# The first product of each seven-product down pair goes into the third bank and is copied; the fourth pair of the last but one batch takes the seven-product form

## The chip, the cores and the metric

The kernel runs on one core of one Trainium2 chip. The metric is the device time of one execution in microseconds (us), as the median of several runs. The core has a matrix engine (PE, with its weight loads listed as PEld), a vector engine (DVE), a scalar engine (ACT), a general engine (POOL) and the DMA queues, most of which are issued from SP. Matmul results land in PSUM, which the program allots in banks of 128 partitions by 512 float32.

## The reference: a gated feed-forward layer with quantised activations and ternary down weights

Inputs are `x` (4 x 1024 x 512, float32), a condition vector per batch (4 x 128), `norm_w` (512 x 128), `up_w` (4096 x 512) and `down_w` (512 x 2048). Cut to what matters:

```python
scale = cond @ norm_w.T + 1.0
h = x * (scale[:, None, :] * rsqrt(mean(x * x) + EPS))
val, gate = split(h @ up_w.T)                 # 2 x 2048 columns
h = val * gelu(gate)
hq = round(h * 127 / max|h| per token) ...    # int8 grid per token
wq = round(down_w / mean|down_w|) in -1, 0, 1 # ternary
y = hq @ wq.T * scales + x
```

## The kernel before, in words

There are four batches of 1024 tokens. Work is written out by hand: the program order of each engine's instructions is the order in which that engine runs them, and the framework puts in the semaphores. The hidden width of 2048 is cut into NJ = 16 blocks of 128. Batch 0 takes the plain up product; batches 1, 2 and 3 take the up product in a seven-product form, one `slot` for each block, so that slots are numbered g = 16 to 63. A slot's up matmuls are 512 wide (L580).

The down product of a batch is done while a later batch is in its slots. It works on tiles of 128 tokens. A `Pair` (L812 and after) takes two tiles, one of each half h of the batch, for the same tile number a (0 to 3), and forms the 2 x 2 block product over the two halves of the 2048 hidden columns and the two halves of the 512 output columns. It takes seven products of eight matmuls each, 256 wide (L851), rather than the 32 matmuls 512 wide of the plain form `down_mm` (L800). The methods are:

- `sum1` and `sums` form four sums of the tokens' blocks on DVE (L827, L834 to L836).
- `first` runs three products: B11, T1 and B21. `third` runs T2, `fourth` runs B22 and T3, `fifth` runs T4. In what follows these are the products' names, with the pair's number a in brackets where it is needed: T1(3).
- Three PSUM banks k1, k2 and k3 are used. The first product is needed in both halves of k1. `first` puts it into the right half and ACT copies it to the left half (L859). `third` has an ACT copy from k1 to k2 (L868) and `fourth` one inside k2 (L877). `onto` (L891) is the DVE instruction that scales a bank, or half a bank, and adds it to the token's `x`.

Batches 0 and 1 are brought down as pairs in slots j = 10 to 13 (`DOWN`) of the batch that follows each, b = 1 and b = 2: eight pairs, whose `first` stands at the slot's start (`early`). Batch 2 is brought down at the very end: pairs 0, 1 and 2 in the seven-product form (`old_first`, `old_third`, `old[a].fourth()`, `old[a].fifth()`), their sums made in the slots j = 10 to 12 of the last batch, and tile number 3 in the plain form, 32 matmuls 512 wide in three pieces of 8, 16 and 8 (`down_mm(b - 1, ...)`). Between these stand the steps of the last batch's own quantisation, for the eight pieces i of 2 blocks of one half h, in the list `work`: `quant_scale` on DVE (L772), and then either a rounding on DVE (L776) or two on ACT (`quant_up` L780 and `quant_down` L784). The last batch's own down product (`po_end`, L800) needs these pieces and ends the kernel.

Of the kernel before, what the change touches and what calls it, by code (L numbers as in the profile page):

```python
# [50 lines left out]
def glu_quant_kernel(  # L51
# [68 lines left out]
    def t_view(b):  # L120
        v = R[:, b % 2].bitcast(F16)[:, : NA * C_ALL * 2 * HALF]
        return v.rearrange("p (a c l k t) -> p a c l k t", a=NA, c=C_ALL, l=2, k=2)
# [16 lines left out]
    def s_tile(g):  # L139


        if g >= NJ:
            return SXY[:, (g + 1) % 2]
        return S_more if g % 3 == 2 else SXY[:, g % 3]

    def h_slots(g, n=1):
        s = g % NSLOT
        return H[:, s : s + n]
# [7 lines left out]
    def bank(tag, bufs, shape=None, name=None):  # L156
        return psum.tile(shape or [P, TOK], F32, name=name or tag, tag=tag, bufs=bufs)
# [416 lines left out]
    def product(c, g, ps, start, stop):  # L574
        s = s_tile(g)[:, PLACE[c]]
        s = s.rearrange("p w (k f) -> p w k f", k=2)
        tv = t_view(g // NJ)
        o = ps.rearrange("p (a t) -> p a t", t=P)
        for n, (w, l, k) in enumerate(TERMS):
            PE.matmul(  # L580
                o, s[:, w, k, :], tv[:, :, c, l, k, :],
                start=start and n == 0, stop=stop and n == len(TERMS) - 1,
                skip_group_check=True,
            )
# [210 lines left out]
    def down_mm(b, h, a, po, js, y0=0, y1=2):  # L795

        q = q_view(b)
        n = NJ // 2
        for j in js:
            PE.matmul(  # L800
                po.rearrange("p (y c o) -> p y c o", c=2, o=P),
                q[:, a, h, j],
                wd8[:, :, j // n, j % n, :, y0:y1].rearrange("p c o y -> p y c o"),
                start=j == 0, stop=j == NJ - 1,
            )
# [6 lines left out]
    class Pair:  # L812
# [23 lines left out]
            DVE.tensor_tensor(self.s[4], a12, self.s[2], ALU.subtract)  # L836
            self.s[3] = a21

        def product(self, w, name, bank, half, start, stop, both=False):


            w = w.rearrange("p (j t) -> p j t", t=P)
            t = w_block(name)
            n = NJ // 2
            for j in range(n):
                m, po = t[:, :, j], bank[:, half * HALF : (half + 1) * HALF]
                po = po.rearrange("p (c o) -> p c o", c=2)
                if both and j == 0:
                    m = m.rearrange("p (y c) o -> p y c o", y=1).to_broadcast([P, 2, 2, P])
                    po = bank.rearrange("p (y c o) -> p y c o", y=2, c=2)  # L850
                PE.matmul(  # L851
                    po, w[:, j], m, start=start and j == 0, stop=stop and j == n - 1,
                    skip_group_check=True,
                )

        def first(self, banks):
            self.banks = k1, _, k3 = banks
            self.product(self.part(0, 0), "B11", k1, 1, True, True, True)
            ACT.copy(k1[:, :HALF], k1[:, HALF:])  # L859
            self.product(self.s[1], "T1", k3, 0, True, True)  # L860
            self.product(self.part(0, 1), "B21", k1, 0, False, True)

# [386 lines left out]
    def add_pieces(dve, act, b, s, pieces, at):  # L1249
        for i, h in pieces:  # L1250
# [9 lines left out]
            cost = 1.29 + (0.8 if (i, h) in BY_VECTOR else 0)  # L1260
            dve.add(at, cost, go, (slot, "z" if (i, h) in BY_VECTOR else "x"))

    def old_places(a):

        if a == 0:
            v = wpool.tile([P, 2, D], F32, name="sq_0", tag="xn", bufs=1)
            u = wpool.tile([P, 4, HALF], F32, name="sr_0", tag="xt", bufs=1)
            return v[:, 0], v[:, 1], u.rearrange("p n d -> p (n d)")[:, :D]
        if a == 1:
            v = wpool.tile([P, C_ALL, 2, HALF], F16, name="sq_1", tag="nx", bufs=1)  # L1270
            v = v.rearrange("p c l d -> p (c l d)").bitcast(F32)
            return [v[:, n * D : (n + 1) * D] for n in range(3)]
        v = h_slots(B * NJ, 2).rearrange("p s h t -> p (s h) t")
        return [v[:, n] for n in range(3)]

    state = {}
    for b in range(1, B):
# [45 lines left out]
        for j in range(NJ):  # L1323
            g = b * NJ + j
            down = b + 1 < B and j in DOWN
            if down:
                pair, a = pairs[j], DOWN[j]
                xrs = [down_load(b - 1, h, a) for h in range(2)]
            early_sums, late_sums = D_SUM_AT.get((b, j), ((), ()))
            left = SLOT_US + PAIR_US * down - OWN_US + 0.4  # L1330
            more = D_SUM_US * len(late_sums) + 0.7 * (j + 1 == min(DOWN) and b + 1 < B)
            left -= D_SUM_US * len(early_sums) + more
            mine = {p: [sum(c[e] for _, c in steps.get((j, p), ())) for e in range(2)] for p in "xyz"}
            left -= sum(mine[p][0] for p in "xyz")
            act_left = {"x": 2.7, "y": 2.2 if down else 1.1, "z": 0}

            def run(p):
                nonlocal left
                for f, _ in steps.get((j, p), ()):
                    f()  # L1340
                if p == "x":
                    cap = min(left, 3.9 - mine["x"][0] - (0 if down else mine["y"][0] + more))
                    left -= cap - dve.run((j, p), cap)
                elif p == "z":
                    left = dve.run((j, p), left)
                if p != "z":
                    act.run((j, p), act_left[p] - mine[p][1])

            def early():
                if down:  # L1350
                    pair.first([po_bank(f"po_{b}_{a}_{n}") for n in range(3)])
                    pair.sums()
                d_sums(early_sums)

            def next_pair():
                if b + 1 < B and j + 1 in DOWN:
                    pairs[j + 1] = Pair(b - 1, DOWN[j + 1])
                    pairs[j + 1].sum1(h_slots(g + 1)[:, 0, 0])

            def more_sums():  # L1360
                next_pair()
                d_sums(late_sums)

            mid = [nothing] * 3
            if j + 1 == min(DOWN):
                mid[0] = more_sums
            if down:
                mid = [lambda: (pair.third(xrs, dq), d_sums(late_sums)), lambda: (pair.fourth(), next_pair()), lambda: (loads(), pair.fifth())]

            def loads():  # L1370
                if NJ + 2 <= g + 2 < B * NJ:
                    s_load_x(g + 2)
                if NJ + 2 <= g + 1 < B * NJ:
                    s_load_y(g + 1)


            def late():
                if b == 1 and j + 1 == min(DOWN):

                    banks = [po_bank(f"po_set_{n}") for n in range(3)]  # L1380
                    PE.matmul(
                        banks[1].rearrange("p (a t) -> p a t", t=P),
                        s_tile(g + 1)[:, 0, 0, :P], t_view(b)[:, :, 0, 0, 0, :],
                        start=True, stop=True,
                    )

            if b + 1 == B and j in DOWN and DOWN[j] < 3:
                pairs[DOWN[j]] = Pair(b - 1, DOWN[j])
                places = old_places(DOWN[j])
                pairs[DOWN[j]].sum1(places[0])  # L1390
                pairs[DOWN[j]].sums(*places[1:])
            if j == 4:
                token_turn(b - 1, am)
            if j == 5:
                bring_dq = token_undo(b - 1, dq)
            if j == 6:
                bring_dq()
            if j == NJ - 1:
                get_ready()
            elif b == 1 and j == 0:  # L1400
                get_ready()
            slot(g, lambda: run("x"), lambda: run("y"), lambda: run("z"), early, mid, late)
            if not down:
                loads()
# [18 lines left out]
            xr = down_load(b - 1, h, a)  # L1423
        old_x[h, a] = xr

    old = [pairs[a] for a in range(3)]

    def old_banks(a):
        if a % 2 == 0:
# [3 lines left out]
    def old_first(a):  # L1433
        old[a].first(old_banks(a))

    def old_third(a):
        old[a].third([old_x[h, a] for h in range(2)], state[b - 1])
# [55 lines left out]
        f()  # L1493
    last_loads()

    pos = [bank("AE"[h], 2, name=f"po_{b}_3_{h}") for h in range(2)]
    down_mm(b - 1, 0, 3, pos[0], range(NJ // 2))
    old[2].fourth()
    for f in work[2:7]:
        f()  # L1500
    down_mm(b - 1, 0, 3, pos[0], range(NJ // 2, NJ))
    down_mm(b - 1, 1, 3, pos[1], range(NJ // 2))
    old[2].fifth()
    down_mm(b - 1, 1, 3, pos[1], range(NJ // 2, NJ))
    for f in work[7:11]:
        f()
    for h in range(2):
        down_end(b - 1, h, 3, pos[h], old_x[h, 3], state[b - 1])
    for f in work[11:]:
        f()  # L1510
    work = [f for _, f in token_scale(1, am)] + [lambda: token_turn(b, am, 1, 2)]
# [56 lines left out]
```

## Time and profile before

| | |
|---|---|
| median of 3 runs | 731.27 us (730.51 to 731.33) |
| profiled execution, its own time | 730.43 us |
| span of that execution, first to last instruction | 728.6 us |
| granted TensorE clock | 1.000 |
| busy: PE, DVE, ACT, POOL | 99%, 80%, 54%, 27% of the span |

The profile counts times from the span's start. A matmul's own duration in it (272 ns for 256 columns, 379 ns for 512) is longer than the distance to the next, since matmuls are pipelined; what a row of eight costs is read from the start of one group to the start of the next. In a line of the timeline stand the start in us, the length, the engine, the source line, the operation, the tile written and the tiles read, the count, and in brackets the idle time before it with what ended it.

### The profile page before, as it was taken

How to read it: one execution, taken by the hardware profiler on the slowest of the kernel's cores; microseconds unless marked ns; L12 is line 12 of the kernel's file. 1: busy time of each engine (PE TensorE's matmuls, PEld its weight loads, DVE VectorE, ACT ScalarE, POOL GpSimd, SP SyncE). 2: the span in 40 equal slices, each digit the busy share in tenths (PEclk: the TensorE clock that was granted, in tenths of full speed). 3: DMA queues.
4: the chain of work that ended last, by engine and by line, in shares of the span. 5: the costliest groups of instructions: out<-in, count | busy, mean ns of one | idle time of the engine just before them, and what ended most of it. 6: DMA issues, size and time to landing. Idle time of an engine off the chain costs nothing.

```text
span 728.6 us, 10140 instructions
## 1 busy us (share of the span) xinstructions
PE 719.9 (99%) x3661; PEld 358.8 (49%) x3661; DVE 581.2 (80%) x819; ACT 396.3 (54%) x629; POOL 196.1 (27%) x207
## 2 busy tenths in 40 slices
PE   7999999999999999999999999999999999999998
PEld 3544444444444446655444445665444444445744
DVE  7877889975698899788689897787678888755897
ACT  6868876772336674444335676543433665332274
POOL 1379887775100033440000030360020000000100
PEclk9999999999999999999999999999999999999999
DMA  6759999988444654876735646866934555452253
GB/s 236 251 172 303 291 273 249 254 199 230 117 102 102 131 155 130 180 186 159 181 101 103 131 101 174 202 144 163 230 96 102 90 114 104 101 102 89 89 188 115
DMA packets 203982, 117.30 MB, mean 161 GB/s; under 512 B 165382, under 2 KB 174487, under 8 KB 203932
## 3 DMA queue, kind: packets, MB, share of 16 engines
q1 hardware_dynamic: 203642, 116.33, 63.8%
q8 instruction: 28, 0.46, 0.2%
q10 hardware_dynamic: 290, 0.33, 0.1%
q14 instruction: 22, 0.18, 0.1%
HBM read 54.22 MB, written 23.09 MB: 106 GB/s over the span
## 4 chain that ended last, share of the span: by engine, by line
PE 96%; DVE 1%; DMA 1%; ACT 0%; issue 0%; SPq 0%; DVEq 0%
PE A L580 34%; PE E L580 17%; PE pg L595 10%; PE pv L595 10%; PE B L580 9%; PE po L851 8%; PE po_end L800 4%; PE po L800 1%; DMA H<-in_x_dram 1%; DMA SXY<-H 1%; PE po_B L851 0%; PE ptx L941 0%; PE pv L638 0%; DVE R L949 0%; PE pw L323 0%; PE pg L638 0%
## 5 line engine op out<-in xcount | busy, mean ns | idle before, releaser
L580 PEld LDWEIGHTS <-SXY 128*128 128x128 f16 x2016 | 197.2, 98 | 232.3 <-issue 0.6
L580 PE MATMUL A<-R,SXY 128*128 128x512 f16 x1152 | 266.2, 379 | 0.0
L580 PE MATMUL E<-R,SXY 128*128 128x512 f16 x576 | 140.0, 379 | 0.1
L678 DVE SCALAR_TENSOR_TENSOR H<-A,sg,t 128x512 f32<-128x512 f32 x48 | 36.0, 750 | 73.4 <-PE A L580 73.2
L730 POOL PARTITION_ALL_REDUCE am<-R x8 | 14.4, 1794 | 230.7 <-DVE R L716 230.7
L772 DVE TENSOR_TENSOR H<-H,am 128x1024 f32<-128x1024 f32 x64 | 76.2, 1216 | 0.0
L595 PEld LDWEIGHTS <-SXY 128*128 128x128 f16 x486 | 47.5, 98 | 57.4 <-DMA SXY<-H 0.8
L691 ACT ACTIVATE t<-t,sg 128x512 f32<-128x512 f32 x48 | 34.6, 721 | 70.1 <-DVE t L688 69.9
L580 PE MATMUL B<-R,SXY 128*128 128x512 f16 x288 | 70.0, 379 | 0.0
L714 DVE TENSOR_REDUCE gm<-H 128x512 f32<-128x1024 f32 x56 | 69.0, 1232 | 1.0
L595 PE MATMUL pg<-R,SXY 128*128 128x512 f16 x252 | 57.8, 379 | 0.3 <-DMA SXY<-H 0.3
L851 PE MATMUL po<-wd,R 128*128 128x256 fp8e4 (+1 forms) x448 | 56.8, 275 | 0.0
L595 PE MATMUL pv<-R,SXY 128*128 128x512 f16 x234 | 54.4, 379 | 0.0
L851 PEld LDWEIGHTS <-R 128*128 128x128 bf16 (+1 forms) x480 | 47.0, 98 | 12.8
L675 ACT ACTIVATE t<-B,sg 128x512 f32<-128x512 f32 x48 | 33.0, 688 | 36.4 <-PE B L580 36.4
L484 POOL TENSOR_SCALAR ssq<-ssq 128x2 f32<-128x2 f32 x12 | 3.6, 299 | 176.8 <-ACT xt L514 124.1
L658 ACT COPY t<-A 128x512 f32<-128x512 f32 x48 | 28.0, 583 | 39.5 <-PE A L580 39.2
L666 ACT COPY B<-A 128x512 f32<-128x512 f32 x48 | 27.4, 572 | 39.0 <-PE A L580 38.6
L780 ACT ACTIVATE H<-H 128x1024 f32<-128x1024 f32 x38 | 39.9, 1050 | 14.1 <-DVE H L772 14.1
L670 ACT COPY v<-E 128x512 f32<-128x512 f32 x48 | 28.1, 586 | 31.3 <-PE E L580 27.8
L716 DVE TENSOR_TENSOR R<-R,gm 128x512 f32<-128x512 f32 x56 | 41.9, 749 | 1.3
L697 DVE SCALAR_TENSOR_TENSOR H<-v,sg,t 128x512 f32<-128x512 f32 x48 | 36.6, 762 | 7.4 <-ACT t L691 7.4
(207 smaller groups left out, 972.5 us busy)
## 6 DMA issues: line engine op xcount, KB each, us to landing
SXY<-s_dram SPq DMA_DIRECT2D x57, 256.0 KB, 3.2
s_dram<-SXY SPq DMA_DIRECT2D x18, 384.0 KB, 3.3
H<-in_L_cond_up_w_dram SPq DMA_DIRECT2D x13, 512.0 KB, 5.6
SXY<-s_dram SPq DMA_DIRECT2D x39, 128.0 KB, 3.3
xr<-in_x_dram SPq DMA_DIRECT2D x19, 256.0 KB, 3.5
out_dram<-xr SPq DMA_DIRECT2D x19, 256.0 KB, 2.6
H<-in_x_dram SPq DMA_DIRECT2D x8, 512.0 KB, 7.9
R<-in_L_cond_down_w_dram SPq DMA_DIRECT2D x8, 512.0 KB, 7.1
```

What stands on the lines that cost most here:

```text
L580: PE.matmul(o, s[:, w, k, :], tv[:, :, c, l, k, :], start=start and n == 0, stop=stop and n == len(TERMS) - 1, skip_group_check=True,)
L595: PE.matmul(ps, a[k // 2][:, w, k % 2, :], XP[:, l, k, h * TOK : (h + 1) * TOK], start=n == 0, stop=n == len(terms) - 1,)
L675: ACT.activation(cur["t1"], pb, AF.Gelu, scale=gain(g, 1))
L678: DVE.scalar_tensor_tensor(h_half(g - 1, 0), prev["A"], gain(g - 1, 0), prev["t1"], ALU.mult, ALU.mult)
L691: ACT.activation(prev["t2"], prev["t2"], AF.Gelu, scale=gain(g - 1, 1))
L697: DVE.scalar_tensor_tensor(h_half(g - 1, 1), prev["v"], gain(g - 1, 0), prev["t2"], ALU.mult, ALU.mult)
L714: DVE.tensor_reduce(gm[0], v, AX.X, ALU.max, apply_absolute_value=True)
L716: return [largest, lambda: DVE.tensor_tensor(m, m, gm[0], ALU.max)]
L772: DVE.tensor_tensor(v, v, r.to_broadcast([P, 2, TOK]), ALU.mult)
L780: ACT.activation(v, v, AF.Copy, bias=MAGIC)
L800: PE.matmul(po.rearrange("p (y c o) -> p y c o", c=2, o=P), q[:, a, h, j], wd8[:, :, j // n, j % n, :, y0:y1].rearrange("p c o y -> p y c o"),
L851: PE.matmul(po, w[:, j], m, start=start and j == 0, stop=stop and j == n - 1, skip_group_check=True,)
```

## The change

In the eleven pairs, and in a new twelfth, the first product goes 256 wide into the right half of the third bank k3, and ACT copies it from there into both halves of k1 with one instruction 512 wide. T1 then goes into the left half of the same bank k3, as it did before. The one matmul in a pair that was 512 wide is gone. Since k1 is then never started by a matmul in a pair, one more matmul is issued, once, in the slot before the first pair.

Tile number 3 of batch 2 becomes a fourth pair. Its sums are made in slot j = 13 of the last batch, in places left over from the other pairs. Its products stand at the end of the kernel in the place of the three pieces of the plain form.

```diff
-        def product(self, w, name, bank, half, start, stop, both=False):
+        def product(self, w, name, bank, half, start, stop):
...
-                if both and j == 0:
-                    m = m.rearrange("p (y c) o -> p y c o", y=1).to_broadcast([P, 2, 2, P])
-                    po = bank.rearrange("p (y c o) -> p y c o", y=2, c=2)
...
         def first(self, banks):
             self.banks = k1, _, k3 = banks
-            self.product(self.part(0, 0), "B11", k1, 1, True, True, True)
-            ACT.copy(k1[:, :HALF], k1[:, HALF:])
+            self.product(self.part(0, 0), "B11", k3, 1, True, True)
+            m1 = k3[:, HALF:].rearrange("p (y o) -> p y o", y=1).to_broadcast([P, 2, HALF])
+            ACT.copy(k1.rearrange("p (y o) -> p y o", y=2), m1)
             self.product(self.s[1], "T1", k3, 0, True, True)
             self.product(self.part(0, 1), "B21", k1, 0, False, True)
...
-        v = h_slots(B * NJ, 2).rearrange("p s h t -> p (s h) t")
-        return [v[:, n] for n in range(3)]
+        if a == 2:
+            v = h_slots(B * NJ, 2).rearrange("p s h t -> p (s h) t")
+            spare.append(v[:, 3])
+            return [v[:, n] for n in range(3)]
+        return [wpool.tile([P, D], F32, name="sq_3", tag="sc", bufs=1), *spare]
...
                     banks = [po_bank(f"po_set_{n}") for n in range(3)]
-                    PE.matmul(
-                        banks[1].rearrange("p (a t) -> p a t", t=P),
-                        s_tile(g + 1)[:, 0, 0, :P], t_view(b)[:, :, 0, 0, 0, :],
-                        start=True, stop=True,
-                    )
+                    for bank in banks[:2]:
+                        PE.matmul(
+                            bank.rearrange("p (a t) -> p a t", t=P),
+                            s_tile(g + 1)[:, 0, 0, :P], t_view(b)[:, :, 0, 0, 0, :],
+                            start=True, stop=True,
+                        )
...
-            if b + 1 == B and j in DOWN and DOWN[j] < 3:
+            if b + 1 == B and j in DOWN:
                 pairs[DOWN[j]] = Pair(b - 1, DOWN[j])
...
     last_loads()
 
-    pos = [bank("AE"[h], 2, name=f"po_{b}_3_{h}") for h in range(2)]
-    down_mm(b - 1, 0, 3, pos[0], range(NJ // 2))
+    old_first(3)
     old[2].fourth()
     for f in work[2:7]:
         f()
-    down_mm(b - 1, 0, 3, pos[0], range(NJ // 2, NJ))
-    down_mm(b - 1, 1, 3, pos[1], range(NJ // 2))
+    old_third(3)
     old[2].fifth()
-    down_mm(b - 1, 1, 3, pos[1], range(NJ // 2, NJ))
     for f in work[7:11]:
         f()
-    for h in range(2):
-        down_end(b - 1, h, 3, pos[h], old_x[h, 3], state[b - 1])
+    old[3].fourth()
+    old[3].fifth()
     for f in work[11:]:
         f()
```

More of the change, by code (lines that the diff above doesn't have):

```diff
@@ L1261, in add_pieces @@
             dve.add(at, cost, go, (slot, "z" if (i, h) in BY_VECTOR else "x"))
+    spare = []
     def old_places(a):
@@ L1267, in old_places @@
             u = wpool.tile([P, 4, HALF], F32, name="sr_0", tag="xt", bufs=1)
-            return v[:, 0], v[:, 1], u.rearrange("p n d -> p (n d)")[:, :D]
+            u = u.rearrange("p n d -> p (n d)")
+            spare.append(u[:, D:])
+            return v[:, 0], v[:, 1], u[:, :D]
         if a == 1:
@@ L1424, in old_load @@
         old_x[h, a] = xr
-    old = [pairs[a] for a in range(3)]
+    old = [pairs[a] for a in range(NA)]
     def old_banks(a):
```

## The prediction

> **What bounds the kernel now.** I read the page's busy times and chain first, then the timeline of one pair in the middle, then the timeline of the end, then the stretches of the end.
>
> ```profile
> PE 719.9 (99%) x3661; PEld 358.8 (49%) x3661; DVE 581.2 (80%) x819; ACT 396.3 (54%) x629; POOL 196.1 (27%) x207
> ...
> PE 96%; DVE 1%; DMA 1%; ACT 0%; issue 0%; SPq 0%; DVEq 0%
> ```
>
> PE bounds nearly everything, so a matmul saved is time saved, and a time in which PE waits is time lost. First, PE at the start of a middle pair (b = 1, a = 0), and ACT in the same stretch:
>
> ```profile
> 274.07 1.14 PE L851 MATMUL po<-wd,R 128*128 128x512 fp8e4 x8
> 275.06 1.04 PE L851 MATMUL po<-wd,H 128*128 128x256 fp8e4 x8
> ```
> ```profile
> 274.62 0.72 ACT L691 ACTIVATE t<-t,sg 128x512 f32<-128x512 f32 x1 [0.71 <-DVE t L688]
> 275.26 0.36 ACT L859 COPY po<-po 128x256 f32<-128x256 f32 x1
> ```
>
> B11 takes 0.98 (274.07 to 275.06), then T1 runs on while ACT copies. The copy begins 0.20 after T1's start, takes 0.36, and is done 0.31 before B21 at 275.93. Nothing waits. Now the end, where the fourth tile's plain matmuls (L800) lie among pair 2's products; PE, ACT and DVE in turn:
>
> ```profile
> 687.92 1.89 PE L800 MATMUL po<-wd,R 128*128 128x512 fp8e4 x8
> 689.65 1.04 PE L851 MATMUL po<-wd,H 128*128 128x256 fp8e4 x8
> 690.52 1.04 PE L851 MATMUL po<-wd,R 128*128 128x256 fp8e4 x8
> 691.40 3.62 PE L800 MATMUL po<-wd,R 128*128 128x512 fp8e4 x16
> 694.85 1.04 PE L851 MATMUL po<-wd,R 128*128 128x256 fp8e4 x8
> ```
> ```profile
> 690.64 1.06 ACT L780 ACTIVATE H<-H 128x1024 f32<-128x1024 f32 x1 [2.98 <-DVE H L772]
> 691.73 1.06 ACT L784 ACTIVATE R<-H 128x1024 bf16<-128x1024 f32 x1
> 692.69 0.37 ACT L877 COPY po<-po 128x256 f32<-128x256 f32 x1
> ```
> ```profile
> 687.95 0.75 DVE L891 SCALAR_TENSOR_TENSOR SXY<-po_B,dq,SXY 128x512 f32<-128x512 f32 x1
> 688.61 0.87 DVE L891 SCALAR_TENSOR_TENSOR SXY<-po,dq,SXY 128x256 f32<-128x256 f32 x2
> 689.39 1.22 DVE L772 TENSOR_TENSOR H<-H,am 128x1024 f32<-128x1024 f32 x1
> ```
>
> The reader is to see L877. Its product T3(2) is through at 691.40, but the copy runs only at 692.69, behind the two roundings of piece 0 that stand before it in ACT's order. It costs nothing, because 16 plain matmuls (3.45) cover it until T4(2) at 694.85. DVE has no gap from 685.3 on; in the busy times by stretch it is the third engine figure:
>
> ```profile
> 700.00:710.00 10.00, 10.00 (x48) 4.54 (x47) 9.90 (x13) 6.04 (x7) 0.00 (x0) 1.00 0.32 97
> ```
>
> **Unit prices.** A product of eight 256-wide matmuls: 0.875 (685.30, 686.18, 687.05, 687.92). A 512-wide matmul: 0.216 (16 in 691.40 to 694.85). ACT's copy of 512 columns between banks:
>
> ```profile
> L666 ACT COPY B<-A x48: 570/570/579, 187.2 to 661.8; 128x512 f32<-128x512 f32 x48
> ```
>
> So 0.57. PE to ACT 0.20 as above; ACT to PE 0.05 (a cast L347 ends at 13.67, the matmul that needs it starts at 13.72).
>
> **Part 1, B11 at 256 wide.** 0.98 becomes 0.875: minus 0.105 a pair.
>
> **Part 2, the copy out of k3.** ACT now reads one half of the bank into whose other half PE wants to write T1 next. May it? No row of before has PE writing half a bank while another engine reads the other half, so both ends stay: no wait, or T1 waits for the whole copy. Nearest is a pair of readers near the start:
>
> ```profile
> 22.16 0.41 DVE L359 TENSOR_TENSOR SXY<-pw,SXY 128x256 f16<-128x256 f32 x1
> 22.61 0.59 ACT L363 COPY H<-pw 128x512 f32<-128x512 f32 x1 [0.34 <-DVE SXY L359]
> ```
>
> Both only read the bank pw and write elsewhere, and yet ACT idled 0.34 until DVE had ended. Two readers have no data to order; the program orders engines on a bank. I take the wait. Its size: 0.20 + 0.57 + 0.05 = 0.82, less 0.105, so plus 0.715 a pair.
>
> The Trainium skill, PSUM — Partial Sum Buffer, section "PSUM bank collisions raise a hardware error", speaks against this change: two engines may not touch one bank on the same partitions at once, disjoint columns included, and semaphores must guard by bank. By it T1 waits in every pair; by addresses alone it would not, and rival one's sum would hold. The L363 row agrees with the page.
>
> Seven of the eight middle pairs pay it: 5.0. ACT is free there when B11 ends (in the pair shown, the gelu ends at 275.34, and B11 is 0.22 later by the added setting matmul). The eighth (b = 1, a = 3) waits already:
>
> ```profile
> 321.66 0.50 PE L851 MATMUL po<-wd,H 128*128 128x256 fp8e4 x3 [0.59 <-DVE H L827]
> ```
>
> Its T1 starts 0.75 after B11's end because of sum1; the two waits overlap, so 0. The setting matmul adds 0.22. Middle: 5.2. Should the copy cost only the 0.36 of the narrow one, each pair is 0.21 cheaper; should a 0.72 gelu stand ahead of it each time, about 0.45 dearer.
>
> **Part 3, sums of the fourth pair.** Four DVE instructions at 0.69 = 2.75, at the start of slot 13 of the last batch. DVE is idle there for 3.76 before L678 at 647.45, so 0; without that cover up to 2.75 late on DVE. Their places are the other pairs' leftovers, and no new wait shows.
>
> **Part 4, the end, in order of time.** Bare matmul time falls: 32 x 0.216 = 6.90 becomes 7 x 0.875 = 6.12, minus 0.78. But the plain pieces were the cover.
>
> Pair 0: ACT is in a gelu from 670.11 to 670.83, so the copy runs 670.79 to 671.36 and T1(0) starts 671.41, not 670.25; shift 1.1 to 1.2. Pairs 1 and 2 add 0.715 each. B11(3) thus starts at 690.5, where 687.92 stood, and ends at 691.4.
>
> Its copy stands on ACT behind the roundings of piece 0. DVE's gapless run is moved by 1.8 with PE (its L688 waits for a slot product, 683.87 to 685.7), so L772 of piece 0 ends at 692.3, the roundings (2.2) at 694.6, the copy at 695.1. T1(3) starts 695.14: PE has waited 3.7.
>
> B21(3), then B22(2) end at 697.8. Only now can DVE do pair 2's `onto` (698.0 to 698.7), and behind it in DVE's order wait L772 for pieces 1, 2 and 3. Piece 1 ends at 699.9, its roundings at 702.2, and only then comes ACT's copy of third(3) (to 702.5). PE, through with T3(2), T2(3) and T4(2) at 700.4, waits 2.1 for B22(3).
>
> T3(3) ends at 704.3. Its copy stands behind the roundings of pieces 3 and 4; piece 4's L772 follows three `onto` on DVE and ends at 705.4, the roundings at 707.7, the copy at 708.0. T4(3), right behind T3(3) with nothing between, has waited 3.8 and ends at 708.9. That is where `po_end` starts, at 697.45 before: plus 11.4. Check: 1.1 + 2 x 0.715 + 3.7 + 2.1 + 3.8 - 0.78 = 11.4.
>
> `po_end` is gapless PE work of 27.7. It would now have its pieces with more to spare than before (half 1's first L772 at about 716 for a need at 722.7), so DVE's two more half-width `onto` (0.87 the two) and the later SP stores cost nothing. The whole 11.4 reaches the end.
>
> **Sum.** 730.43 + 5.2 + 11.4 = 747.0 for a profiled execution; the median lies 0.84 above that execution: 747.9.
>
> The Trainium skill, TensorE: Matmul & The Clock Gate, Part 1, says that PE idle for a window of about 3.4 us drops to half clock. By it, as an estimate, each of the two longest waits could cost 1.7 more, which would make 751.3. The longest PE wait of before is 1.5 and all slices have clock 1.00, so no run here shows it; the sum leaves it out.
>
> **Rivals.** *One, order by address:* T1 runs on, B21 is due 0.875 after B11 and needs 0.82, no wait. Middle: -8 x 0.105 + 0.22 = -0.6. At the end B21(3) still waits for a copy behind the roundings: 0.4 + 3.0 + 2.1 + 3.8 - 0.8 and the rest of pairs 0 to 2, about 8.8. Time 739.5. Against it: the L363 row.
>
> *Two, bank waits only:* DVE and ACT catch up during them, and the copies of the fourth pair find ACT free. 11 x 0.715 + 0.22 - 0.78 - 0.7, plus 0.20 + 0.36 + 0.05 for T4(3) behind T3(3): 738 to 739. Against it: DVE's 9.90 of 10.
>
> *Three, faster:* neither wait, because ACT takes the fourth pair's copy at once. It decides at L772 of piece 0: its roundings, 2.2, would have to be over at 689.0, when B11(3)'s copy is due, so L772 would have to end by 686.8; it ended at 690.61. Price: 12 pairs' saving is 11 x 0.105 + 0.78 - 0.22 = 1.7, of which the end lets through about 0.3, since ACT's last rounding of piece 3 of half 1 ends at 715.44 for a need at about 715.7. Between -0.9 and -1.7: 729.6 to 730.4.
>
> **How the numbers follow.** Main case 0.87; one 0.06; two 0.04; three 0.02; no change 0.01. Main alone: 12 copies at the cheap or dear end move it by -2.3 or, in the eight middle pairs, +3.6, and the end's three waits by about 2 either way, since they hang on DVE's order. Both seldom add, so 743.5 to 752.0, which leaves out the rivals and a tenth of the main case, under 2 in 10. A measurement tells 0.2% (1.5 us) from no change: faster 0.02, same 0.01, slower 0.97.
>
> **What would show it.** Right: T1's PE rows (L851) wait on ACT for about 0.6 to 0.8 in each pair; L859's successor is 0.57 long; near 691 to 708 PE stands still three times, for 3.7, 2.1 and 3.8, each until an ACT copy behind L784; `po_end` starts near 714 (708.9 + 5.2). Wrong: T1 following B11 with no gap; `po_end` starting before 706; DVE idle where I have it full.

## The result, and the profile after

The changed kernel takes 751.68 us (median of 6 runs, 749.98 to 753.74) beside 730.98 us for the kernel before (6 runs, 730.51 to 731.33). The ratio is 1.0285, with a 95% interval of 1.0269 to 1.0301: slower by 20.7 us. The profiled execution shown here has a span of 750.7 us and took 752.44 us.

The page of the kernel after, the same two parts as were shown of before, and the granted clock in 40 slices:

```profile
PE 724.5 (97%) x3686; PEld 363.2 (48%) x3686; DVE 584.9 (78%) x825; ACT 399.7 (53%) x632; POOL 195.7 (26%) x207
...
PEclk9999999999999999999999999999999999999899
...
PE 4%; ACT 0%; DVE 0%; issue 0%
```

PE's share falls from 99% to 97%, and one slice near the end shows a granted clock below 0.9. The chain that ended last now reaches back only to the end of the kernel (PE 4% in place of 96%). TensorE's own waits are therefore the view to read: PE's waits by what ended them, in total, with their number and the longest.

```profile
PE po L848 <- ACT po L857: 4.4, 6, 1.1
PE po_E L848 <- ACT po_B L857: 4.3, 2, 3.7
PE po_A L848 <- ACT po_A L875: 3.7, 1, 3.7
...
PE po L848 <- DVE H L697: 2.6, 4, 0.7
PE po_B L848 <- ACT po_A L866: 1.8, 1, 1.8
```

For the kernel before, this list has one line of a pair only, of 0.6. L857 is the copy that was L859, L866 and L875 were L868 and L877, and the products' line L851 is now L848. The four waits put down to DVE's L697 stand at T1 of other pairs and are just as long (0.66 each), so I read them as waits for L857 too. A middle pair's start, first PE and then ACT (b = 1, a = 0):

```profile
275.62 1.04 PE L848 MATMUL po<-wd,R 128*128 128x256 fp8e4 x8
277.31 1.03 PE L848 MATMUL po<-wd,H 128*128 128x256 fp8e4 x8 [0.66 <-ACT po L857]
```
```profile
275.95 0.72 ACT L691 ACTIVATE t<-t,sg 128x512 f32<-128x512 f32 x1 [0.72 <-DVE t L688]
276.69 0.57 ACT L857 COPY po<-po 128x512 f32<-128x512 f32 x1
```

T1 starts 1.69 after B11 instead of 0.98: 0.875 for B11, 0.20 to the copy at 276.69, 0.57 for the copy, 0.05 back to TensorE. The end of the kernel, PE and then ACT:

```profile
696.89 1.04 PE L848 MATMUL po_E<-wd,R 128*128 128x256 fp8e4 x8
701.59 1.87 PE L848 MATMUL po_E<-wd,sq 128*128 128x256 fp8e4 x8 [3.66 <-ACT po_B L857]
703.25 1.91 PE L848 MATMUL po_B<-wd,R 128*128 128x256 fp8e4 x8
704.95 1.91 PE L848 MATMUL po<-wd,H 128*128 128x256 fp8e4 x8
...
711.34 1.03 PE L848 MATMUL po_B<-wd,H 128*128 128x256 fp8e4 x8 [1.85 <-ACT po_A L866]
...
716.92 1.82 PE L848 MATMUL po_A<-wd,R 128*128 128x256 fp8e4 x8 [3.67 <-ACT po_A L875]
```
```profile
698.91 1.06 ACT L780 ACTIVATE H<-H 128x1024 f32<-128x1024 f32 x1 [2.27 <-DVE H L772]
699.99 1.06 ACT L784 ACTIVATE R<-H 128x1024 bf16<-128x1024 f32 x1
700.96 0.58 ACT L857 COPY po_B<-po_E 128x512 f32<-128x512 f32 x1
...
709.97 1.06 ACT L784 ACTIVATE R<-H 128x1024 bf16<-128x1024 f32 x1
710.93 0.37 ACT L866 COPY po_A<-po_B 128x256 f32<-128x256 f32 x1
...
715.54 1.06 ACT L784 ACTIVATE R<-H 128x1024 bf16<-128x1024 f32 x1
716.50 0.37 ACT L875 COPY po_A<-po_A 128x256 f32<-128x256 f32 x1
```

The copy of the fourth pair's first product follows the two roundings without a gap, and T1(3) follows the copy. The copies that end the two later waits stand behind a rounding in the same way. T1(3), B21(3) and B22(2) then take 1.7 each where a product takes 0.875. The busy times of two stretches, the granted clock being the figure before the last two, say why:

```profile
701.59:706.66 5.07, 5.07 (x25) 3.57 (x24) 0.00 (x0) 0.00 (x0) 0.00 (x0) 0.50 0.94 322
716.92:720.50 3.58, 3.58 (x13) 1.91 (x13) 1.67 (x3) 0.00 (x0) 0.00 (x0) 0.52 0.22 82
```

After each of the two waits of 3.7, TensorE runs at half clock: the granted clock is 0.50 and 0.52 in these stretches.

### The profile page after: what moved, and what is told of

It reads as the page before. It is cut to its first block, busy times and chain, and to the rows that moved or that the text cites. A ratio compares the mean times of both kernels' runs of the same rounds, so it can differ in the third digit from the quotient of the medians.

```text
span 750.7 us, 10208 instructions
## 1 busy us (share of the span) xinstructions
PE 724.5 (97%) x3686; PEld 363.2 (48%) x3686; DVE 584.9 (78%) x825; ACT 399.7 (53%) x632; POOL 195.7 (26%) x207
## 5 line engine op out<-in xcount | busy, mean ns | idle before, releaser
L848 PEld LDWEIGHTS <-R 128*128 128x128 bf16 (+1 forms) x512 | 50.9, 99 | 16.4 <-issue 3.8
L848 PE MATMUL po<-wd,R 128*128 128x256 fp8e4 x448 | 55.8, 273 | 0.0
L697 DVE SCALAR_TENSOR_TENSOR H<-v,sg,t 128x512 f32<-128x512 f32 x48 | 37.9, 790 | 7.4 <-ACT t L691 7.4
```

Of the source, the lines that this page charges most:

```text
L697: DVE.scalar_tensor_tensor(h_half(g - 1, 1), prev["v"], gain(g - 1, 0), prev["t2"], ALU.mult, ALU.mult)
L848: PE.matmul(po, w[:, j], m, start=start and j == 0, stop=stop and j == n - 1, skip_group_check=True,)
```

## The experiments

The theory is the prediction's: T1 waits for ACT's copy because both are on one bank, the fourth pair's copies wait behind roundings in ACT's order, and, new, about 4 us come from the clock. Each run was timed beside the kernel before on the same chip: the first four beside 731.26, the last three beside 731.57.

**One part alone: the firsts.** The changed kernel with the fourth tile back in the plain form.

```diff
-            if b + 1 == B and j in DOWN:
+            if b + 1 == B and j in DOWN and DOWN[j] < 3:
...
-    old_first(3)
+    pos = [bank("AE"[h], 2, name=f"po_{b}_3_{h}") for h in range(2)]
+    down_mm(b - 1, 0, 3, pos[0], range(NJ // 2))
...
```

> Part 1 and 2 of the change alone: the first product goes into the third bank and is copied in all eleven pairs, and the fourth tile of the last but one batch stays in the plain form. My theory (T1 waits for the copy because both are on one bank, and the other half of the loss is the fourth pair's copies queued behind roundings): eight middle pairs 5.1, three pairs at the end 2.5, time 738.6 us, no stretch at a lower clock, since no wait is longer than 1.3. Rival (the loss is all in the fourth pair): 731 us or a little less.

Measured: 739.01 us, ratio 1.0101 (1.0075 to 1.0128), clock 1.000. It costs 7.75 us, where the sum had 7.6. The rival falls.

**The other part alone: the fourth pair**, with the first product of before.

> The fourth pair alone, with the first product of before (512 wide once, copied inside the first bank). My theory: T1(3) runs on, but B21(3) waits about 2.7 for ACT's copy behind the roundings of piece 0, B22(3) 2.1, T4(3) 3.8; less 0.8 for the matmuls saved: plus 8.5 at full clock, 739.5 us, and up to 2 more if the wait of 3.8 brings a stretch at half clock; so 739.5 to 741.5. Rival (the waits at the end come only from T1 and the copy sharing a bank): 730 to 731 us.

Measured: 741.38 us, ratio 1.0137 (1.0108 to 1.0166), 10.1 us. PE's waits in this run:

```profile
PE po_A L851 <- ACT po_A L877: 3.7, 1, 3.7
PE po_B L851 <- ACT po_B L859: 2.4, 1, 2.4
PE po_B L851 <- ACT po_A L868: 1.9, 1, 1.9
...
PE po_B L851 <- DVE SXY L891: 0.7, 1, 0.7
```

The three waits for ACT are there with no bank shared between copy and T1, so the shared bank does not make them. That ACT's order does is tested for the first of them further down; for the other two it is read from the timeline, and no run moved their copies alone. The first is now B21(3)'s and lasts 2.4 only; after it the clock is still 1.00 (1.00 from 692 to 705 us, 0.66 from 705 to 710 after the wait of 3.7). The fourth line is a wait of this run's own: B11(3) waits for DVE to release its bank.

The two parts alone add up to 17.9 us, and together they cost 20.7. In the profiled executions, sharing the bank makes the first wait of the end begin one product earlier (3.66 in place of 2.35), half clock follows it and costs 2.5, and the wait of 0.7 for DVE goes away. How long a wait has to be for the clock to fall is not shown: one of this run's four executions, the one of 742.82, has a mean clock of 0.993 where the other three have 0.998.

**Another bank for the copy.** As the firsts alone, but with the first product in the second bank.

```diff
-            self.product(self.part(0, 0), "B11", k3, 1, True, True)
-            m1 = k3[:, HALF:].rearrange("p (y o) -> p y o", y=1).to_broadcast([P, 2, HALF])
+            self.product(self.part(0, 0), "B11", k2, 1, True, True, True)
+            m1 = k2[:, HALF:].rearrange("p (y o) -> p y o", y=1).to_broadcast([P, 2, HALF])
             ACT.copy(k1.rearrange("p (y o) -> p y o", y=2), m1)
             self.product(self.s[1], "T1", k3, 0, True, True)
...
+        return [k1, k3, k2] if len(turns) % 2 else [k1, k2, k3]
```

> As the firsts alone, but the first product goes into the second bank (its first matmul 512 wide, as before) and is copied from there into both halves of the first with the same 512-wide ACT instruction, while T1 goes into the third bank as ever; the second and third bank change places from pair to pair, so that the first product finds a bank that is long free. My theory (T1 waits because ACT reads the bank that T1 writes): no wait before T1, B21 is not late either (0.82 against 0.875), 731.0 to 731.6 us with the one setting matmul more. Rival (T1 waits for the copy for another reason, such as where the semaphore stands, or the copy itself is too long): as the firsts alone or more, 738.5 to 739.5 us.

Measured: 733.40 us, ratio 1.0031 (1.0018 to 1.0044). The first middle pair again, PE and ACT:

```profile
274.20 1.14 PE L851 MATMUL po<-wd,R 128*128 128x512 fp8e4 x8
275.18 1.04 PE L851 MATMUL po<-wd,H 128*128 128x256 fp8e4 x8
276.06 1.04 PE L851 MATMUL po<-wd,R 128*128 128x256 fp8e4 x8
```
```profile
275.38 0.57 ACT L860 COPY po<-po 128x512 f32<-128x512 f32 x1
```

The same 512-wide copy runs from 275.38 to 275.95, T1 runs on beside it from 275.18, and B21 at 276.06 is not late. No pair's row waits for L860. So it is the shared bank that holds T1, and neither the copy's length nor its place. The 2 us over my 731.0 to 731.6 are a wait of my own making: T1's bank is now one that the pair before releases last, and in two middle pairs DVE is late with it.

```profile
PE po L851 <- DVE xr L892: 2.1, 2, 1.1
```

**The waits filled.** The changed kernel with matmuls of no use in the three waits of the end.

```diff
             self.product(self.part(0, 0), "B11", k3, 1, True, True)
+            if fill:
+                fill()
...
-    old_first(3)
+    old_first(3, lambda: busy(15))
...
+    busy(7)
     old[3].fourth()
+    busy(16)
     old[3].fifth()
```

> The changed kernel with 15, 7 and 16 matmuls of no use put into the three waits of the fourth pair at the end, into a spare bank, so that TensorE is not idle there; they are shorter than the waits (3.2, 1.5 and 3.5 against 3.8, 2.0 and 3.8). My theory (about 4 us of the change's loss is the clock at half speed after those waits): clock 1.00 throughout and 4 us less than the changed kernel, 747.5 us. Rival (the slow matmul rows there are no clock effect, or the clock falls all the same): no difference, 751.7 us, or more if the added matmuls get in the way.

Measured: 747.72 us, ratio 1.0217 (1.0193 to 1.0240), clock 1.000, against 751.68. Adding 38 matmuls takes 4.0 us away (4.2 if each is set against its own runs of before). The products after the first wait are again 0.87 apart:

```profile
700.93 1.03 PE L848 MATMUL po_E<-wd,sq 128*128 128x256 fp8e4 x8 [0.41 <-ACT po_B L859]
701.80 1.04 PE L848 MATMUL po_B<-wd,R 128*128 128x256 fp8e4 x8
702.67 1.04 PE L848 MATMUL po<-wd,H 128*128 128x256 fp8e4 x8
```

T1(3) still starts 4.69 after B11(3), for 4.70 in the changed kernel, and T4(3) 4.70 after T3(3), for 4.71, so these copies come no earlier. So 4 us of the loss are the clock, and most of the 16.5 that remain are the waits themselves.

**The copy ahead of the roundings.** One move in the changed kernel.

```diff
+    old_first(3)
     for f in work[1:2]:
         f()
     last_loads()
 
-    old_first(3)
     old[2].fourth()
```

> The changed kernel with one move: the fourth pair's first part (its products and its copy) stands ahead of the two roundings of piece 0 in the order of the end, so that ACT runs the copy before them. My theory (the 3.7 before T1(3) is the copy queued behind the roundings, and half clock follows from it): that wait falls to the 0.7 of the other pairs, the slow stretch after it (2.5) goes too, the waits of 1.9 and 3.7 that follow stay: 751.7 - 2.9 - 2.5 = 746.3 us. Rival (the copy waits for a bank or for DVE, not for its place in ACT's queue): no change, 751.7 us.

Measured: 747.28 us, ratio 1.0218 (1.0204 to 1.0232). That is 4.4 us less than the changed kernel, or 5.0 if each is set against its own runs of before (15.7 and 20.7 above them), where I had 5.4.

```profile
698.27 1.03 PE L848 MATMUL po_E<-wd,sq 128*128 128x256 fp8e4 x8 [0.66 <-ACT po_B L857]
...
705.53 1.03 PE L848 MATMUL po_B<-wd,H 128*128 128x256 fp8e4 x8 [1.86 <-ACT po_A L866]
...
711.10 1.86 PE L848 MATMUL po_A<-wd,R 128*128 128x256 fp8e4 x8 [3.66 <-ACT po_A L875]
```

The first wait, of 3.66, has become the 0.66 of every other pair, and the other two stay. The rival falls. In the profiled execution the one long wait that is left costs more in clock than either did before: the granted clock is 0.50 from 710.0 to 716.5, and T4(3) and `po_end` lose 2.8 by it.

**The firsts, covered.** As the firsts alone, but T1 and B21 come later: in the middle after the slot's first up product, at the end after another pair's or the slot's product.

```diff
             ACT.copy(k1.rearrange("p (y o) -> p y o", y=2), m1)
+
+        def rest(self):
+            k1, _, k3 = self.banks
             self.product(self.s[1], "T1", k3, 0, True, True)
             self.product(self.part(0, 1), "B21", k1, 0, False, True)
...
             ACT.copy(pb, cur["A"])
+            second()
```

> The firsts alone, fourth tile plain, but with other work of TensorE between the first product and T1: the slot's first up product in the middle pairs, and products of the neighbouring pair or of the slot at the end. No matmul is 512 wide in a pair. My theory (the copy from the third bank is free once 0.9 us of matmuls that do not touch that bank lie behind the first product): no wait, 11 x 0.105 less, 0.22 more for the setting matmul: 0.9 to 1.0 us less than before, 730.2 us, ratio 0.9987. Rival (T1 is held by something else too, or ACT's longer copy delays the slot): no gain, 731.2 us or more, up to 738.6.

Measured: 729.82 us beside 731.57, ratio 0.9980 (0.9971 to 0.9989), 1.75 us less; the expected 0.9987 lies in the interval. A middle pair of it:

```profile
276.58 1.04 PE L850 MATMUL po<-wd,R 128*128 128x256 fp8e4 x8
277.46 1.46 PE L580 MATMUL A<-R,SXY 128*128 128x512 f16 x6
278.75 1.04 PE L850 MATMUL po<-wd,H 128*128 128x256 fp8e4 x8
```

The up product takes the 1.29 in which ACT copies (277.66 to 278.23), and T1 follows without a wait. This version beats both kernels. The bare matmuls were worth 0.9 of the 1.75; the interval reaches from 0.8 to 2.1, and nothing here says whether the rest is more than noise.

This trace also holds a stretch at half clock near its start, before any pair, behind a wait that is shorter than those of the end:

```profile
PE ptx L944 <- DVE H L939: 2.2, 1, 2.2
```
```profile
10.00:15.00 5.00, 3.54 (x20) 3.45 (x20) 3.35 (x16) 2.03 (x4) 2.29 (x3) 0.72 0.65 247
```

The wait of 2.19 ends at 11.46, and the clock is 0.50 from 12.5 to 15.5. In the changed kernel's trace the same wait is 2.79 long, and the clock is 1.00 over the first 20 us.

**Everything covered.** The firsts as in the last run, and the fourth pair in an order of its own.

```diff
+    old_first(3)
     old[1].fifth()
+    old[3].rest()
+    work[1]()
...
+            if h == 0 and j == 0:
+                old[3].fifth()
```

> Both parts of the change in an order without the waits: the firsts covered as in the run before; the fourth pair in the seven-product form with its copies ahead of the roundings in ACT's order, each copy covered by another pair's product, and T4(3) behind the first eight matmuls of the last batch; its first bank is one of the two-buffered ones. My theory (what the fourth pair saves on TensorE is then lost again, since DVE and ACT, 0.9 us of added half-width scaling included, become late for the last batch's pieces): clock 1.00, waits of about 0.4 to 0.8 each at three pieces of the last batch, in all 731.2 us, no gain over before. Rival (TensorE alone counts): 731.2 - 1.0 - 0.8 = 729.4 us.

Measured: 731.72 us beside 731.57, ratio 1.0007 (0.9996 to 1.0018): no difference, and 1.9 us more than with the firsts covered alone. What PE waits for at the end is new, while DVE is as full as it was (third engine figure of the stretch):

```profile
PE po_end L802 <- ACT R L786: 1.2, 2, 1.0
```
```profile
700.00:710.00 10.00, 9.85 (x46) 4.13 (x43) 9.86 (x12) 6.58 (x8) 0.00 (x0) 1.00 0.15 48
```

The last batch's product now waits for ACT's second rounding, which hangs on DVE: ACT stands idle for 1.97 until L774 on DVE has ended, just ahead of the roundings that the longer wait is for. The expectation had waits at three pieces; there were two. So this order does not bring in the fourth pair's 0.78 of matmul time: DVE and ACT are no earlier for it, and DVE has 0.9 more to do. Other orders were not tried.

## Why the prediction was right

The forecast was slower, 747.9 in a range of 743.5 to 752.0; measured, 751.68. Its steps, read from the two profiled executions, whose spans differ by 22.1 (750.7 less 728.6):

| stretch | predicted | measured |
|---|---|---|
| before the first pair, without the setting matmul | 0 | 1.3 |
| middle pairs and setting matmul | 5.2 | 5.1 |
| pairs 0 to 2 at the end, to B11(3) | 2.5 | 2.5 |
| B11(3) to the start of `po_end` | 8.9 | 12.1 |
| `po_end` and after | 0 | 1.0 |

The measured column is the shift of the same instruction from one trace to the other: B11 of the first pair from 274.07 to 275.62 (0.22 of it the setting matmul), of the first pair at the end from 669.27 to 675.72, B11(3) from 687.92 to 696.89, `po_end` from 697.45 to 718.53. The 1.3 ahead of the first pair lies before anything that the change touches (the wait ahead of the `ptx` matmuls near the start is 2.8 in the trace after and 1.5 in that of before; over all nine traces it goes from 0.9 to 2.8); the profiled execution is also 0.8 above its median. I count it as no part of the change's cost.

*Part 1 and 2* held to a tenth: 0.82 less 0.105 a pair, and nothing in the pair (b = 1, a = 3) that had waited for its sums anyway: T1 of that pair is 3.64 later than before, T1 of the pair ahead of it 3.68. The doubt whether T1 must wait at all is settled by the copy from another bank. The rule of the Trainium skill, PSUM — Partial Sum Buffer, section "PSUM bank collisions raise a hardware error", gave the same verdict as the row of two readers. What the chip does if T1 is not held was not tried, and k2 and k3 are different tiles as well as different banks, so these runs show that sharing the bank makes the program wait, not what the wait averts.

*Part 3*: no wait of TensorE in slot 13 showed, and DVE is still idle for 1.10 behind the four sums.

*Part 4* held in its mechanism, place and order: three waits of 3.66, 1.85 and 3.67 in the lines, for 3.7, 2.1 and 3.8, each ended by the copy that was named. The term that was mis-sized is the clock, which the sum put at nothing. The products between the first and second wait lost 2.5 (four of them, 701.59 to 707.59, took 6.0 for 3.5), T4(3) 0.7 (1.61 for 0.875), and `po_end` most of its 1.0. That is 4.2 in the trace, and 4.0 by the run with the waits filled.

That the range held is in part luck. It was made of copies that might cost less or more and of waits that might move by 2; none of these moved by more than a few tenths. What brought the time to 751.68, 0.3 short of the range's upper end, was the clock, for which the range had no room of its own.

The prediction had cited the Trainium skill, TensorE: Matmul & The Clock Gate, Part 1, for half clock after some 3.4 us of idleness, and left it out of the sum because no row of before showed it. At the end of the kernel the runs agree with it: all four waits of 3.66 or 3.67 were followed by half clock, waits of 1.85, 1.86 and 2.35 were not. At the start they do not: half clock came after a wait of 2.19 in one trace and not after one of 2.79 in another. So the length of the wait does not decide alone. The estimate worked out from the page, 751.3, was nearer than the sum. It was too low for the first stretch: half clock lasted at least 5.07 us after the first wait, not 3.4, and so cost 2.5 and not 1.7.

The rivals: *one* (order by address) fell with the firsts alone, 739.0 and not 731; *two* (bank waits only) fell with the fourth pair alone, which has the queue waits and no bank wait; *three* (faster) named as its limit that the end would let through little of the saved matmul time, and the run with everything covered agrees with that.

## What to carry to other kernels

A matmul saved counts only if the copy that pays for it finds cover. Look at which bank the copy reads, put work on another bank behind the product it reads, and put the copy ahead of longer work in its engine's order. Plain work between dependent pieces is cover: before it is made faster, list what it hides. Look at the granted clock behind every long wait of TensorE: each of the four waits of 3.7 us here cost 1.7 to 2.8 us more than itself.

## What the runs showed of the hardware that I had not expected

Half clock came twice in one execution that had a single core running, each time with a wait of 3.7 us. The first time it set in 2 us into the wait and the granted clock was 0.50 from 700.0 to 706.5; the second time it set in only when TensorE was at work again, and was 0.50 from 717.0 to 720.0. 38 matmuls of no use, in those waits and the one between them, made the kernel 4.0 us faster. The length of a wait did not settle whether the clock fell: it fell with 2.19 at the start of one trace, and did not with 2.35 at the end of a second and with 2.79 at the start of a third. Two parts of a change that cost 7.7 and 10.1 alone cost 20.7 together, and 2.5 of that is a stretch at half clock that neither part has alone in its trace.
